# One set of quantising scales per strip, its stages divided and placed anew, and early copies moved to ScalarE, in the first layer of a two-layer kernel

## The chip, the cores and the metric

The kernel runs on one core of one Trainium2 chip. The metric is the device time of one execution in microseconds (us), the median of several runs. Five engines work side by side, each with its own queue of instructions: PE (TensorE, matmuls and transposes; its weight loads are shown apart as PEld), DVE (VectorE), ACT (ScalarE), POOL (GpSimd) and SP (SyncE, which issues transfers here).

## The reference

Two layers run one after the other on an input of 2 x 2048 tokens with 256 features. The change is in the first. It adds to the input a gated linear attention and a linear map with quantised operands, both of the normalised input; the second layer (an attention with position biases, and eight experts of which each token takes two) isn't touched. Cut to the first layer:

```python
def _gla_scan(q, k, v, g):
    def step(S, inp):
        qt, kt, vt, gt = inp
        S = jnp.exp(gt)[..., None] * S + kt[..., None] * vt[..., None, :]
        ot = jnp.einsum('bhd,bhde->bhe', qt, S)
        return (S, ot)
...
def _L0_attn_ref(x, W_in, W_out, W_g1, W_g2, ln_w):
    u = x @ W_in.T
    v, q, lg = jnp.split(u, 3, axis=-1)
    q = jax.nn.silu(q)
    f = jax.nn.sigmoid(lg)
    k = 1.0 - f
    g = jax.nn.log_sigmoid(lg)
    o = _gla_scan(tohead(q), tohead(k), tohead(v), tohead(g))
    gate = jax.nn.sigmoid(x @ W_g1.T @ W_g2.T)
    o = o * gate
    mu = jnp.mean(o, axis=-1, keepdims=True)
    var = jnp.var(o, axis=-1, keepdims=True)
    o = (o - mu) * jax.lax.rsqrt(var + LN_EPS) * ln_w
    return o @ W_out.T
...
def _mx_quantize(t, eps=1e-30):
    blocks = t.reshape(rows, K // BLOCK_SIZE, BLOCK_SIZE)
    scales = jnp.maximum(jnp.max(jnp.abs(blocks), axis=-1) / FP6_E2M3_MAX, eps)
    q = _nearest_on_grid(blocks / scales[..., None], _GRID)
    return (q, scales)
...
xn = _layernorm(x, axis=-1)
x = x + _L0_attn_ref(xn, ...) + _L0_ffn_ref(xn, ...)
```

Blocks of 32 neighbouring values share a scale: their greatest absolute value divided by 7.5. Each value divided by its scale is rounded to the nearest point of a six-bit grid and multiplied by the scale again, for the input and for the weight of the linear map.

## The kernel before

**Strips.** `layer0` (L517) works through the 4096 tokens in eight strips of 512, four to each of the two sequences. A strip's tokens lie as four tiles of 128 tokens by 256 features. An object `Strip` holds what belongs to one strip, and its methods issue the work of one step:

- `norm_x` normalises the input into `xn` (two buffers): statistics L133, L135, the power on POOL L142, the result L144; `columns_x` transposes it on PE into `xnT`.
- `values_gates` (L640) multiplies `xnT` by a joint weight, one 128x512 PSUM tile `vf_ps` for each of four token tiles. Its first half is the values, copied to `v` by ACT (L653); its second half the logits, copied to `logit` by DVE (L652). After each second tile, ACT takes Exp (L656) and Ln (L657) of two tiles together into `soft`.
- `queries_begin` and `queries_end` make the queries: `q_ps` and `c_ps` on PE, `ls` and `spans` on ACT, `arg` (L705) and `q` (L708) on DVE.
- `keys` subtracts the logits from `k_ps` (DVE, L727) and takes Exp (ACT, L730) into `kt`; `key_columns` transposes `kt` into `k_tr` on PE and copies it to `k` by DVE (L764), 128x512 for each of two heads.
- `gates` and `gates_end` make the gate (`g1T` and L748 to L750 on ACT).
- `weights` makes the products `a_ps` of keys and queries and masks them (DVE, L786).
- `chunk(n)`, n from 0 to 3, runs the recurrence over 128 tokens: `o_ds_ps` on PE, the new `state` (DVE, L844; ACT L842 where a sequence begins), `kept` (ACT, L809), the gated result `og` (DVE, L853) and its statistics.
- `norm_o`, `columns_o`, `sum_up`, `norm_2`, `columns_2` normalise and transpose the result, add both maps to the input (`y_ps` on PE, L882 on DVE) and prepare what the second layer reads: `queries_keys`, `values`, `greatest`.

**Quantising.** `mx_steps` (L163) quantises 512 values per partition, half a strip: scales on DVE (the reduction L182 to `amax`, L184 `scale`, L186 `rscale`, L188 `nscale`), then on DVE the division L190, the power of two L194 and L197, and two roundings L199 and L202, then POOL L205. This first stage ends with a `yield`. The second stage is L207 on DVE and L208 on POOL, with another `yield`; the third is L210 on DVE and L211 on POOL, which multiplies by `nscale` and leaves the result in `mx_v`. Work tiles `pw`, `r` and `nr` have one buffer each, `nscale` and `mx_v` two. `Strip.quantise` (L659) runs the two halves one after the other. Between them is no `yield`: a step that ends the first half also does the scales and the first stage of the second. So five steps do a strip. `quantised_columns` transposes the result on PE into `xdT`. The weight is quantised once, by the same stages, at the start (`quantised_weight`, L602).

**Order.** The loop at L926 writes out by hand which step follows which: strip `now` runs through its recurrence while strip `after` is prepared, `later` is normalised and `before` is handed to the second layer. `next(quantise)` marks where one step of quantising is put. PE's instructions are kept in this order (`keep_in_program_order`, named `pin`). On the other engines only pinned instructions stay in order among themselves: L207, L210 and `arg` L705 always; in `quantise(begin=pin)`, for strips 0 and 1, also the reduction L182; and for the first `norm_x` calls the first statistics. The framework's scheduler places the others by its own reckoning of when they are ready, with the source order as priority, so that DVE's rows in the trace stand among each other in another order than in the source.

**Where the steps of quantising stand.** Strip 0: the first after `keys`, the second after `key_columns`, the third after `weights`, the fourth after strip 1's `values_gates`, the fifth after `chunk(0)`. Strip 1, in the pass of strip 0: one after `quantised_columns` (before `chunk(2)`), one after `queries_end`, one after `chunk(3)`, one after `keys`, the last after `gates`. Later strips, in the pass of the strip ahead of each: after `values_gates`, after `chunk(0)`, after `chunk(1)`, after `queries_end`, after `chunk(3)`.

## Time and profile before

| | |
|---|---|
| median of 3 runs | 1642.38 us (1642.37 to 1642.56) |
| profiled execution | 1642.09 us |
| its span, first to last instruction | 1640.3 us |
| first layer, to the last `norm_ps` | some 433 us |
| busy: PE / PEld / DVE / ACT / POOL | 1583.8 / 1297.9 / 730.3 / 743.9 / 391.2 us |
| mean granted TensorE clock | 0.989 |
| the chain that ended last | PE 86%, DVE 9%, POOL 2%, ACT 1% |

The profile gives each group of instructions by source line, engine and operation, with the tile that it writes and those it reads. What the change touches, between 22 and 150 us:

| row | mean |
|---|---|
| DVE L182 `mx_amax`, 128x16 from 128x512 | 669 ns |
| DVE L190 `mx_v`, 128x512 | 686 ns |
| DVE L652 `logit`, 128x256 from PSUM | 415 ns |
| DVE L764 `k`, 128x512 from PSUM | 672 ns |
| ACT L653 `v`, 128x256 from PSUM | 370 ns |
| ACT L589 `xnT`, 128x512 from PSUM | 586 ns |
| ACT L656 `soft`, Exp, 128x512 from SBUF | 633 ns |

In rows of time, the first number is the start in us from the span's start, the second the duration. Square brackets give how long the engine was idle ahead of an instruction and what ended that wait. The chain of waits is followed back from the last instruction, at each step to what released it. A row that ends in `x8` stands for eight instructions in a row.

### The profile page before, as it was taken

The numbers are of one execution on the slowest core, as the hardware profiler recorded it, in microseconds if no ns is written. First come the engines' busy times: TensorE is split into PE (matmuls) and PEld (weight loads), VectorE is DVE, ScalarE is ACT, GpSimd is POOL, SyncE is SP. The second block draws the span as 40 slices with busy tenths as digits, with TensorE's granted clock in tenths as the row PEclk, the third lists the DMA queues.
The fourth block names the chain that finished last, engine by engine and source line by source line (L and its number), as shares of the span: only waits on it lengthen the run. The fifth ranks groups of instructions, "written<-read, shape, count | busy, mean of one in ns | idle before, by whom it ended". The sixth has DMA issues, their size and how long they took to land.

```text
span 1640.3 us, 33123 instructions
## 1 busy us (share of the span) xinstructions
PE 1583.8 (97%) x13786; PEld 1297.9 (79%) x13786; DVE 730.3 (45%) x2274; ACT 743.9 (45%) x1445; POOL 391.2 (24%) x350
## 2 busy tenths in 40 slices
PE   7789999999999999999999999999999999999996
PEld 4556676667688887888888888988898898888886
DVE  7888676664478866444353222222222222222221
ACT  4344554653688888998987211111111111111110
POOL 4333222211200003233331122222222232222221
PEclk9999999999899999999999999999999999999998
DMA  9710111313540402621126555555565565556531
GB/s 268 187 38 29 54 53 43 93 45 80 149 57 3 84 13 66 142 65 62 58 97 246 180 177 177 180 183 174 180 205 198 164 215 195 171 170 196 177 90 19
DMA packets 82511, 204.42 MB, mean 125 GB/s; under 512 B 8624, under 2 KB 64304, under 8 KB 71728
## 3 DMA queue, kind: packets, MB, share of 16 engines
q0 software_dynamic: 24944, 138.33, 26.0%
q1 hardware_dynamic: 56304, 62.71, 14.2%
q8 instruction: 110, 1.80, 0.5%
q10 hardware_dynamic: 1104, 1.18, 0.2%
q14 instruction: 49, 0.40, 0.1%
HBM read 152.26 MB, written 49.92 MB: 123 GB/s over the span
## 4 chain that ended last, share of the span: by engine, by line
PE 86%; DVE 9%; POOL 2%; ACT 1%; DMA 1%; issue 1%; POOLq 0%; SPq 0%; DVEq 0%; ACTq 0%
PE h_ps L2206 29%; PE y_ps L2222 14%; PE sc L1801 12%; PE o_ps L1823 10%; PE vf_ps L533 3%; PE y_ps L533 3%; PE f_ps L1785 2%; PE tr L583 2%; PE vg_ps L533 2%; PE qk_ps L533 1%; PE g_ps L533 1%; PE q_ps L533 1%; PE o_tr L1758 1%; PE o_ds_ps L533 1%; PE x_ps L2184 1%
## 5 line engine op out<-in xcount | busy, mean ns | idle before, releaser
L2206 PE MATMUL h_ps<-va,qk 128*128 128x256 f32 (+1 forms) x2368 | 484.5, 365 | 0.0
L2206 PEld LDWEIGHTS h_ps<-va,qk 128*128 128x128 f32 x2368 | 425.6, 190 | 53.6 <-issue 0.3
L1807 ACT ACTIVATE pt<-sc,shift 128x512 f32<-128x512 f32 (+3 forms) x687 | 403.8, 704 | 52.3 <-ACT pt L1807 27.1
L2211 ACT ACTIVATE sg<-h_ps 128x256 f32<-128x256 f32 (+1 forms) x296 | 109.2, 369 | 600.5 <-PE h_ps L2206 592.9
L2212 DVE TENSOR_TENSOR larger<-sg,h_ps 128x256 f32<-128x256 f32 (+1 forms) x296 | 119.2, 403 | 359.1 <-ACT sg L2211 359.1
L1801 PE MATMUL sc<-qk 32*128 32x128 f32 (+6 forms) x3916 | 222.5, 336 | 1.6 <-PE norm_ps L533 1.1
L1801 PEld LDWEIGHTS sc<-qk 32*128 32x128 f32 x3916 | 184.1, 186 | 35.3 <-ACT pt L1807 17.0
L1823 PE MATMUL o_ps<-pt,va 128*32 128x128 f32 (+6 forms) x3916 | 188.3, 319 | 3.4 <-DVE o_sb L114 3.4
L1823 PEld LDWEIGHTS o_ps<-pt,va 128*32 128x32 f32 x3916 | 140.6, 110 | 34.3 <-issue 9.6
L2231 POOL DMA_INDIRECT out<-va,to x69 | 109.9, 1592 | 211.0 <-DMA out<-va,to 85.4
L114 DVE TENSOR_TENSOR pt<-pt,keepmask 128x128 f32<-128x128 f32 (+3 forms) x546 | 119.7, 276 | 73.7 <-ACT pt L1807 71.8
L2222 PE MATMUL y_ps<-qk,larger 128*128 128x256 f32 x560 | 124.6, 379 | 0.1
L2227 DVE SCALAR_TENSOR_TENSOR va<-y_ps,wt,half_bias 128x256 f32<-128x256 f32 x69 | 30.4, 479 | 208.5 <-PE y_ps L2222 208.5
L2222 PE MATMUL y_ps<-larger 128*128 128x256 f32 x544 | 120.4, 379 | 0.0
L2222 PEld LDWEIGHTS y_ps<-qk,larger 128*128 128x128 f32 x560 | 104.7, 190 | 13.8 <-DVE larger L2212 0.5
L2222 PEld LDWEIGHTS y_ps<-larger 128*128 128x128 f32 x544 | 102.0, 190 | 13.1
L2116 POOL DMA_INDIRECT table<-rows,place x64 | 67.7, 1057 | 186.0 <-DMA table<-rows,place 149.4
L2146 POOL DMA_INDIRECT qk<-in_wgateup,wrow x37 | 36.7, 991 | 190.4 <-PE h_ps L2206 157.7
L533 PE MATMUL vf_ps<-qk,xnT 128*128 128x512 f32 x128 | 59.2, 617 | 0.0
L533 PEld LDWEIGHTS vf_ps<-qk,xnT 128*128 128x128 f32 x128 | 24.4, 196 | 29.6 <-issue 27.3
L114 DVE COPY o_sb<-o_ps 128x256 f32<-128x256 f32 x64 | 26.9, 422 | 42.1 <-PE o_ps L1823 41.8
L2146 POOL DMA_INDIRECT qk<-in_wdown,wrow x19 | 18.4, 968 | 110.2 <-PE y_ps L2222 83.6
(248 smaller groups left out, 1712.2 us busy)
## 6 DMA issues: line engine op xcount, KB each, us to landing
xb<-table SPq DMA_DIRECT2D x32, 265.0 KB
qk<-qk SPq DMA_DIRECT2D x32, 256.0 KB
qk<-qk SPq DMA_DIRECT2D x64, 128.0 KB
table<-spare SPq DMA_DIRECT2D x3, 2120.0 KB
va<-v SPq DMA_DIRECT2D x4, 1208.0 KB
v<-v SPq DMA_DIRECT2D x8, 574.0 KB
normed<-xn SPq DMA_DIRECT2D x8, 512.0 KB
rows<-normed POOLq DMA_DIRECT2D x16, 256.0 KB, 3.3
```

The costliest lines, as they stand in the source:

```text
L114: return lambda *a, **k: self.tc.keep_in_program_order(begin(*a, **k))
L533: tc.keep_in_program_order(nc.tensor.matmul(*args, **kwargs))
L1801: nc.tensor.matmul(scs[r][:, at : at + q1 - q0], lhsT=heads[rows, 1, kb * P : (kb + 1) * P], rhs=heads[rows, 0, qt * QT + q0 : qt * QT + q ...
L1807: nc.scalar.activation(pt[:, r, 0:width], scs[r][:, 0:width], AF.Exp, bias=shift)
L1823: nc.tensor.matmul(o_ps[r * HR : (r + 1) * HR, to + q0 : to + q1], lhsT=values[b, way][:, kb, h * VC : h * VC + HR], rhs=pt[:, r, at : at ...
L2116: self.nc.gpsimd.indirect_dma_start(out=self.c.table, in_=rows[:, n, :], in_offset=None, out_offset=bass.IndirectOffsetOnAxis(ap=to[:, 2 * ...
L2146: e.nc.gpsimd.indirect_dma_start(out=w, out_offset=None, in_=e.a[name], in_offset=bass.IndirectOffsetOnAxis(ap=e.c.wrow[:, self.b : self.b ...
L2206: nc.tensor.matmul(ps[:, j, rows], lhsT=self.wgu[:, j, c, f * P : (f + 1) * P], rhs=self.xT[:, c, rows], start=c == 0, stop=c == 1,)
L2211: nc.scalar.activation(sg, ps[:, 0, rows], AF.Silu)
L2212: nc.vector.tensor_tensor(self.hT[:, f, rows], sg, ps[:, 1, rows], ALU.mult)
L2222: nc.tensor.matmul(ps[:, c, :], lhsT=self.hT[:, fc, c * P : (c + 1) * P], rhs=self.wd[:, fc, :], start=fc == 0, stop=fc == NFC - 1,)
L2231: nc.gpsimd.indirect_dma_start(out=out, out_offset=bass.IndirectOffsetOnAxis(ap=self.to[:, c : c + 1], axis=0), in_=y[:, c, :], in_offset= ...
```

## The change

Three things change, all in the first layer.

- The scales leave `mx_steps` and become a function of their own, `mx_scales`. For a strip they are made once, for all 1024 values per partition (32 blocks), and each half takes its part. `rscale` now has two buffers. The weight's scales are made as before. What `begin` pins in `mx_steps` is now the division, and in `mx_scales` the reduction.
- `Strip.quantise` has a step of its own for the scales, and a `yield` between the halves, so that seven steps do a strip: scales, then three stages for each half. The loop's `next` calls are placed for them. Strip 0: scales and first stage after `keys`, and after `weights` both the end of the first half and the first stage of the second; the rest stands as before. Strip 1: scales after `quantised_columns`, the first half's stages after `queries_end` and after `chunk(3)` and, with the first stage of the second half, after `keys`; the last two after `gates`. Later strips: scales and first stage after `values_gates`, second stage after `chunk(0)`, third after `chunk(1)`; the second half's stages after `queries_end`, after `chunk(3)` and after `norm_o`.
- For strips 0, 1 and 2 (`early`) ACT copies the logits and the transposed keys, in place of DVE, and takes Exp of each tile straight from PSUM, four of 128x256 instead of two of 128x512.

```diff
+def mx_scales(nc, pool, src, begin=lambda ins: ins):
+    nb = src.shape[1] * E // 32
     amax = pool.tile([P, nb], F32, tag="mx_amax", name="mx_amax")
-    begin(nc.vector.tensor_reduce(amax, blocks(x), AX.X, ALU.max, apply_absolute_value=True))
+    blocks = src.rearrange("p c e -> p (c e)").rearrange("p (b k) -> p b k", k=32)
+    begin(nc.vector.tensor_reduce(amax, blocks, AX.X, ALU.max, apply_absolute_value=True))
     scale = pool.tile([P, nb], F32, tag="mx_scale", name="mx_scale")
     nc.vector.tensor_scalar(scale, amax, 1.0 / 7.5, 1e-30, ALU.mult, ALU.max)
-    rscale = pool.tile([P, nb], F32, tag="mx_rscale", name="mx_rscale")
+    rscale = pool.tile([P, nb], F32, tag="mx_rscale", name="mx_rscale", bufs=2)
     nc.vector.reciprocal(rscale, scale)
     nscale = pool.tile([P, nb], F32, tag="mx_nscale", name="mx_nscale", bufs=2)
     nc.vector.tensor_scalar(nscale, scale, -1.0, None, ALU.mult)
-    nc.vector.tensor_tensor(
+    return rscale, nscale
+
+def mx_steps(nc, pool, src, v, scales, pin=lambda ins: ins, begin=lambda ins: ins):
...
+    rscale, nscale = scales
+    begin(nc.vector.tensor_tensor(
         blocks(v), blocks(x), rscale.unsqueeze(2).to_broadcast([P, nb, 32]), ALU.mult
-    )
+    ))
...
+            self.early = s < 3
...
-                nc.vector.tensor_copy(self.logit[:, n, :], ps[:, E:])
-                nc.scalar.copy(self.v[:, n, :], ps[:, 0:E])
+                if self.early:
+                    nc.scalar.activation(self.soft[:, n, :], ps[:, E:], AF.Exp, scale=-1.0)
+                    nc.scalar.copy(self.v[:, n, :], ps[:, 0:E])
+                    nc.scalar.copy(self.logit[:, n, :], ps[:, E:])
+                else:
+                    nc.vector.tensor_copy(self.logit[:, n, :], ps[:, E:])
+                    nc.scalar.copy(self.v[:, n, :], ps[:, 0:E])
                 if n % 2:
                     part = self.soft[:, n - 1 : n + 1, :]
-                    nc.scalar.activation(part, self.logit[:, n - 1 : n + 1, :], AF.Exp, scale=-1.0)
+                    if not self.early:
+                        nc.scalar.activation(
+                            part, self.logit[:, n - 1 : n + 1, :], AF.Exp, scale=-1.0
+                        )
                     nc.scalar.activation(part, part, AF.Ln, bias=1.0)
 
-        def quantise(self, **how):
+        def quantise(self, begin=lambda ins: ins):
             self.xd = []
+            scales = mx_scales(nc, p1, self.xn, begin)
+            yield
             for i in range(2):
                 v = p1.tile([P, 2 * E], F32, tag="mx_v", name="mx_v", bufs=2)
                 self.xd.append(v.rearrange("p (c e) -> p c e", e=E))
-                for _ in mx_steps(
-                    nc, p1, self.xn[:, 2 * i : 2 * i + 2, :], v, pin, **how
-                ):
-                    yield
+                nb = 2 * E // 32
+                yield from mx_steps(
+                    nc, p1, self.xn[:, 2 * i : 2 * i + 2, :], v,
+                    [t[:, i * nb : (i + 1) * nb] for t in scales], pin, begin,
+                )
+                yield
...
-                nc.vector.tensor_copy(self.k[:, h, :], ps.rearrange("p n t -> p (n t)"))
+                copy = nc.scalar.copy if self.early else nc.vector.tensor_copy
+                copy(self.k[:, h, :], ps.rearrange("p n t -> p (n t)"))
...
     now.keys()
     next(quantise)
+    next(quantise)
     now.gates_end()
...
         now.weights()
         if not before:
             next(quantise)
+            next(quantise)
         if after:
             after.values_gates()
         if before:
             quantise = after.quantise() if after else iter(())
+            next(quantise, None)
         next(quantise, None)
         now.chunk(0)
         next(quantise, None)
         now.chunk(1)
-        if before:
-            next(quantise, None)
-        else:
-            for _ in quantise:
-                pass
+        next(quantise, None)
...
         now.norm_o()
         if before:
+            next(quantise, None)
             before.queries_keys()
         else:
             after.keys()
             next(quantise)
+            next(quantise)
             after.gates()
-            for _ in quantise:
-                pass
+        for _ in quantise:
+            pass
         now.columns_o()
```

## The prediction

> **What bounds the kernel now.** I first split the profiled execution (1642.09 us; its span is 1640.3) into the stages of the first layer. The stretches view gives, for each, PE busy, PEld, DVE, ACT, POOL (all us), then the granted clock.

> ```profile
> 21.00:54.00 33.00, 30.96 (x167) 20.83 (x166) 27.37 (x66) 20.81 (x46) 11.85 (x9) 1.00 0.97 257
> 54.00:89.00 35.00, 27.38 (x143) 21.00 (x142) 29.67 (x81) 12.77 (x25) 12.68 (x10) 0.85 0.45 122
> 89.00:147.40 58.40, 50.35 (x229) 33.88 (x229) 50.97 (x151) 24.25 (x51) 19.29 (x15) 0.94 0.11 40
> 147.40:196.40 49.00, 47.42 (x250) 33.69 (x250) 35.46 (x97) 25.94 (x54) 13.10 (x10) 1.00 0.13 45
> 294.30:342.20 47.90, 47.50 (x251) 33.77 (x252) 30.47 (x85) 26.07 (x55) 9.73 (x8) 1.00 0.23 72
> ```

> From 147 us on PE is busy 96 to 99% of each strip, and the rest of the kernel is PE too (97% of the span). Between 54 and 147 us PE idles 7.6 + 8.1 us, at a granted clock of 0.85 and 0.94, while DVE is busy 85 to 87%. So a gain can come from there almost alone. Next, the chain of waits in that stretch: it runs on DVE and POOL, and PE appears again only at 86.16.

> ```profile
> 66.09 0.61 DVE mx_r L207
> 66.77 1.38 POOL mx_r L208
> 68.17 0.69 DVE mx_nr L210
> 68.86 0.61 DVE mx_amax L182
> 69.49 0.60 DVE mx_scale L184
> 70.11 0.25 DVE mx_rscale L186
> 70.41 0.70 DVE mx_v L190
> ...
> 76.99 0.70 DVE mx_nr L210
> ...
> 79.56 1.03 POOL ln_rstdx L142
> 80.62 1.38 DVE xn L144 x4
> 82.00 0.66 DVE ln_st L133 x2
> 82.74 0.57 DVE k L764
> 83.41 0.57 DVE k L764
> ...
> 86.16 1.64 PE tr L583 x8
> ```

> Both things that the change takes off DVE, the second half's scales and the key copies, stand on this chain. Last, PE's own rows with the waits ahead of them:

> ```profile
> 47.49 0.49 PE L533 MATMUL o_ds_ps<-state,q 128*128 128x128 f32 x2 [1.25 <-ACT state L842]
> 111.33 0.49 PE L533 MATMUL o_ds_ps<-state,q 128*128 128x128 f32 x2 [3.86 <-DVE state L844]
> 167.57 0.49 PE L533 MATMUL o_ds_ps<-state,q 128*128 128x128 f32 x2 [1.28 <-DVE state L844]
> 216.63 0.49 PE L533 MATMUL o_ds_ps<-state,q 128*128 128x128 f32 x2 [1.73 <-DVE state L844]
> ```

> PE waits for the recurrence's state, and DVE is late with it because it holds stages of the quantising ahead of it.

> **A, to 54 us.** Strip 1's four logit copies (DVE, 0.42 each) no longer stand between `vf_ps` and ACT. Now ACT's last `v` copy starts at 46.28, 2.3 us after PE's last `vf_ps`, and state L842 behind it ends at 47.4. ACT's new work per `vf_ps` tile is an Exp, a `v` copy and a logit copy of 128x256 from PSUM. The nearest row, `v<-vf_ps`, is 0.37, so 3 x 0.37 + half an Ln of 0.63 = 1.43 us, under the 1.72 us in which PE makes a tile (four matmuls, 7.1 us for 16). An Exp of this shape is not in the trace: its bounds are 0.26 (spacing of the piped `v` copies) and 0.63 (the Exp of 128x512), and I take the copy's 0.37. ACT keeps pace, and PE's wait of 1.25 us goes. Against it, strip 0's two key copies (0.58 each by `xnT<-tr`, the same shape) join ACT at 34 us, where it is full from 31.2 to 36.7 with gates and `xnT`, for which PE's `vf_ps` at 37.05 waits. Cost 0 (if they fall behind `xnT`, `a_ps` then waits) to 1.16; I take 0.4. **A = -1.25 + 0.4 = -0.85**, bounds -1.3 to +1.2.

> [...] No run here shows the new Exp yet.

> **B, 54 to 89 us.** Scales: per half reduce 0.67, scale 0.17, reciprocal 0.25, negation 0.11. One set for 1024 elements instead of two: the wide reduce is not in the trace; it lies between 0.67 (free width) and 1.34 (double), I take 1.27 (+0.6), the 32-wide rest as before. So strip 1's chain loses the second set, from 68.78 to 70.40, 1.6 us, and DVE pays 0.6 earlier, near 52, where it has 0.21 us idle and is otherwise full: net -1.0. The first half's stage (L190, L194, L197, L199, L202: 2.9 us, from 53.89) moves from in front of chunk 2 to behind `queries_end`. State n=2, run at 56.15 although its `ds_ps` is done at 54.36, can go about 1.5 us earlier, and with it og. DVE's work up to L207 at 66.0 stays the same sum; the wait of 1.07 us for POOL's `rstdo` at 64.4 can now be filled by that stage. I take -0.9, so that L207 comes that much sooner; bounds -1.5 and +4.2 (all of the 2.9 and the 1.27 of POOL L205 exposed). This cost is zero only because L205, done at 58.44, waits 7.6 us for its reader now; without that cover it is the 4.2. Key copies of strip 1: 0.57 x 2 leave the chain, and ACT, idle from 69.1 to 79.5 us, takes them when `k_tr` ends at 77.5: -1.2. **B = -1.0 - 0.9 - 1.2 = -3.1**, bounds -5 and +3.

> **C, 89 to 147 us.** Here DVE is the bound, 87% busy with long waits in it (L207 takes 2.39 at 100.75 beside POOL's `acc` of 2.36; nscale 1.14 at 109.28 beside POOL L205). Off DVE go four logit copies (1.65), two key copies (1.28), a set of small scale steps (about 0.5): 3.4 us. In source the second half's stage now stands behind chunk 2 and the query tail. The unpinned rows of DVE do not follow the source (an `mx_amax` for a later strip stands at 110.34, just ahead of state at 110.94), so I grant only that state, ready from about 106, passes L202, nscale and amax (0.67 + 1.14 + 0.6 = 2.4 of the 3.86 us wait). A shorter wait also keeps PE's clock: the first 8 `qk_ps` after it take 5.29 us, the next 8 3.60; I take 0.8 of the 1.7. Of the 3.4 us I count 0.8 on top, since the last copies (139.3) are behind the transpose that PE waits for. **C = -2.4 - 0.8 - 0.8 = -4.0**, bounds -8 (all of PE's idle) and 0.

> **D, 147 to 390 us.** PE idle: 1.58, 1.72, 1.81, 0.40, 1.08 us in five strips, 6.6 in all. Each strip has DVE waiting for POOL L211 ahead of nscale (0.94 at 164.99), as its two buffers are both in use; with one nscale per strip the buffer is free long before. But L202 waits for the same POOL row through `nr`. If state passes the L202, scale and amax rows (165.07 to 166.48) the wait goes; if not, a wide amax costs 0.6 more. I take -0.8 in each of three strips: **-2.5**, bounds +3 and -5. No DMA is moved, and SP and POOL's queue get nothing new. POOL L205 may come closer to `rstdo` (172.31), 5.1 us after it is free now: covered.

> **Sum.** -0.85 - 3.1 - 4.0 - 2.5 = -10.4: 1642.1 - 10.4 = 1631.7. The median of the runs is 0.3 above the profiled execution, so 1632; for pieces that overlap (an idle gap closes once) I take 1 off the gain: **1633**.

> **Rivals.** (1) *The moves come to nothing*: DVE's order stays by readiness, only removed work counts. A -0.85, B -1.0 - 1.2, C -2 (logits and small steps), D 0: -5, **1637**. For it: the floating rows named above. Against: in strip 1 the stages are pinned. (2) *Nothing reaches PE*: what DVE saves is idle elsewhere, ACT takes 0.4; **1641.5**. Against it: key copies and scales stand on the chain itself. (3) *Slower: the late second half.* Stages stand behind `queries_end`, on DVE ahead of og's normalising. In strip 0 the uncovered 4.2 us; in each of six later strips the whole stage of 2.9 instead of the 1.7 that stands there now (L188 to L182, 164.99 to 166.48, rounded up): +1.2 x 6 = 7.2. With A and the sure gains of B (-3.0): +8.4, **1650**. It decides when the `tr` of og starts over 20 us after the last `vf_ps` of a strip; strip 1's takes 18.9 now (156.34 to 175.21). For it: og's last piece (175.53) already stands behind an L207. Against: DVE has 13 us idle in such a strip.

> **How the numbers follow.** Forecast 0.52 (its own range 1626 to 1637), rival 1 0.20, rival 2 0.08, rival 3 0.20. A measurement here can tell about 0.2%, 3.3 us, from no change; forecast and rival 1 are faster by more: 0.72; rival 2 is within: 0.08; rival 3: 0.20. The range reaches from 1625 to 1645: below it lie C and D at their bounds together, above it most of rival 3.

> **What would show it.** Strip 0: PE's `tr` of `xn2` at 86.16 comes near 82; the chain has no `k` L764 row before it. PE's 1.25 us wait for L842 is gone, and the 3.86 us one is under 2. By 147.4 some 8 us are gained; the later strips take under 49 us each. I am wrong if ACT, not PE, ends the `vf_ps` stretches, if L207 of strip 1's first half comes after 66 us, or if the time after the first layer changes its length.

## The result, and the profile after

| | before | after |
|---|---|---|
| median, same chip | 1642.55 us (1642.1 to 1646.11, 12 runs) | 1643.26 us (1639.32 to 1648.44, 12 runs) |
| profiled execution: run / span | 1642.09 / 1640.3 us | 1644.31 / 1642.5 us |

The ratio after to before is 0.9993, with a 95% interval of 0.9982 to 1.0005: no change that this kernel's measurement can tell. The forecast was 1633 us. The page of the changed kernel, its span, TensorE's work, the granted clock in 40 slices and the chain that ended last:

```profile
span 1642.5 us, 33089 instructions
...
PE 1587.1 (97%) x13786; PEld 1300.2 (79%) x13786; DVE 719.9 (44%) x2224; ACT 751.5 (46%) x1469; POOL 389.7 (24%) x350
...
PEclk9899999999899999999999999999999999999998
...
PE 89%; DVE 7%; POOL 2%; DMA 1%; issue 1%; ACT 1%; POOLq 0%; SPq 0%; DVEq 0%; ACTq 0%
```

VectorE did lose 10.4 us of work and ScalarE gained 7.6 (from 730.3 and 743.9). The end did not follow. The same stretches as in the prediction, cut at this kernel's strips (columns: length, busy us of PE, PEld, DVE, ACT, POOL, then the granted clock):

```profile
21.00:54.00 33.00, 31.97 (x181) 22.19 (x180) 24.28 (x56) 22.82 (x55) 12.57 (x9) 1.00 0.97 252
54.00:88.50 34.50, 25.21 (x125) 19.71 (x125) 27.92 (x77) 12.51 (x24) 13.13 (x10) 0.80 0.49 131
88.50:145.10 56.60, 48.73 (x230) 33.75 (x227) 46.84 (x136) 26.80 (x59) 19.81 (x15) 0.97 0.12 42
145.10:194.00 48.90, 47.98 (x251) 33.77 (x250) 34.23 (x93) 26.02 (x54) 13.04 (x10) 1.00 0.13 45
290.40:339.30 48.90, 47.98 (x249) 33.77 (x248) 30.21 (x81) 26.07 (x54) 9.59 (x8) 1.00 0.23 70
```

The first stretch is better (PE 31.97 of 33 us). In the second PE still idles 9.3 us and its clock is lower than before (0.80, it was 0.85). The third is 1.8 us shorter. The later strips are longer: 48.90 where the strip at 294 us took 47.9.

To place the difference, the table gives the start of each strip's first `a_ps` matmul, of the second layer's first `sc` matmul and of the last part's first `h_ps`, in us from the first instruction. "Later strips" is from strip 2's `a_ps` to `sc`.

| profile | strip 0 | strip 1 | strip 2 | `sc` | strip 1 takes | later strips | `sc` to `h_ps` |
|---|---|---|---|---|---|---|---|
| before | 35.16 | 87.73 | 147.32 | 434.43 | 59.59 | 287.11 | 459.08 |
| before, again (r_before) | 34.70 | 87.49 | 147.88 | 435.07 | 60.39 | 287.19 | 457.48 |
| after | 34.43 | 87.27 | 145.09 | 432.62 | 57.82 | 287.53 | 463.36 |
| after, again (r_after) | 34.29 | 87.11 | 144.92 | 432.38 | 57.81 | 287.46 | 459.27 |
| after, again (r2_after) | 33.52 | 86.34 | 144.16 | 430.69 | 57.82 | 286.53 | 457.43 |

The first layer gave 1.8 us in the pair of profiles at hand, and 1.8 to 4.4 over all pairs of these five. Part of that is the start ahead of strip 0's `a_ps`, which varies from one execution to the next: over the 17 profiles of this document it came anywhere from 33.44 to 35.24 us, and the same order of work up to there gave 33.52 us in r2_after and 35.10 in e_fill. Counted from strip 0's `a_ps` to `sc`, the change gave 1.1 us in this pair and 1.1 to 3.2 over all pairs. The second layer has the same instructions in the same order on every engine, and its length differs by 6 us between executions of one program (457.43 to 463.36). What little the first layer gave is lost in that.

### The profile page after: what moved, and what is told of

Its sections match the earlier page's. It is cut to its first block, busy times and chain, and to the rows that moved or that the text cites. A ratio compares the mean times of both kernels' runs of the same rounds, so it can differ in the third digit from the quotient of the medians.

```text
span 1642.5 us, 33089 instructions
## 1 busy us (share of the span) xinstructions
PE 1587.1 (97%) x13786; PEld 1300.2 (79%) x13786; DVE 719.9 (44%) x2224; ACT 751.5 (46%) x1469; POOL 389.7 (24%) x350
## 4 chain that ended last, share of the span: by engine, by line
PE 89%; DVE 7%; POOL 2%; DMA 1%; issue 1%; ACT 1%; POOLq 0%; SPq 0%; DVEq 0%; ACTq 0%
PE h_ps L2229 29%; PE y_ps L2245 14%; PE sc L1824 12%; PE o_ps L1846 10%; PE vf_ps L540 3%; PE y_ps L540 3%; PE f_ps L1808 2%; PE tr L590 2%; PE vg_ps L540 2%; PE g_ps L540 2%; PE qk_ps L540 1%; PE q_ps L540 1%; PE o_tr L1781 1%; PE o_ds_ps L540 1%; PE x_ps L2207 1%; PE k_ps L540 1%
## 5 line engine op out<-in xcount | busy, mean ns | idle before, releaser
L1824 PE MATMUL sc<-qk 32*128 32x128 f32 (+6 forms) x3916 | 226.0, 337 | 2.0 <-PE norm_ps L540 1.1
```

Of the source, the lines that this page charges most:

```text
L1824: nc.tensor.matmul(scs[r][:, at : at + q1 - q0], lhsT=heads[rows, 1, kb * P : (kb + 1) * P], rhs=heads[rows, 0, qt * QT + q0 : qt * QT + q ...
```

## The experiments

All times are against the kernel before on the same chip, in four comparisons, whose medians for the kernel before were 1639.1, 1638.93, 1641.14 and 1642.83 us. The ratios are those on record; the quotient of the two medians differs from them by up to 0.0013.

| kernel | median us | ratio to before, 95% | strip 1 at | strip 1 takes | later strips | `sc` |
|---|---|---|---|---|---|---|
| e_copies | 1639.87 | 1.0001 (0.9991, 1.0011) | 85.72 | 58.45 | 287.09 | 431.26 |
| e_nocopies | 1644.53 | 1.0025 (1.0013, 1.0038) | 91.50 | 59.69 | 287.54 | 438.73 |
| e_strip1 | 1636.98 | 0.9975 (0.9963, 0.9987) | 85.15 | 57.81 | 286.46 | 429.42 |
| e_later | 1635.45 | 0.997 (0.996, 0.9981) | 87.73 | 59.08 | 283.15 | 429.96 |
| e_both | 1633.68 | 0.9958 (0.9945, 0.997) | 85.23 | 57.89 | 283.01 | 426.13 |
| e_fill | 1638.1 | 0.9986 (0.9977, 0.9994) | 87.93 | 56.56 | 286.46 | 430.95 |
| r2_after | 1639.4 | 0.9991 (0.9982, 1.0001) | 86.34 | 57.82 | 286.53 | 430.69 |
| e_scales | 1639.39 | 0.9991 (0.9981, 1.0) | 87.92 | 62.06 | 283.34 | 433.32 |
| e_best | 1631.55 | 0.9939 (0.9925, 0.9953) | 85.38 | 58.00 | 281.91 | 425.29 |
| e_pin | 1627.68 | 0.9916 (0.9901, 0.9932) | 85.55 | 50.37 | 286.01 | 421.93 |
| e_after_pin | 1639.14 | 0.9981 (0.9971, 0.9991) | 86.71 | 49.98 | 294.55 | 431.24 |
| e_before_pin | 1639.46 | 0.9972 (0.996, 0.9984) | 87.35 | 51.24 | 290.55 | 429.14 |
| e_top | 1629.98 | 0.9915 (0.9898, 0.9933) | 86.61 | 50.34 | 285.49 | 422.44 |

**Both kernels once more, and the parts alone.** r_before and r_after are the two kernels unchanged, in a later comparison, one run each (1641.15 and 1640.19 us).

> The kernel before once more, for a second profile of it. First theory: the first layer repeats itself (first score matmul of the second layer at 434.4 us, within 0.5), and the second layer, the same instructions in the same order in both kernels, varies by some us from one execution to the next (1205.9 us from that matmul to the end in the first profile). Rival: the second layer is as steady as the first, and takes 1205.9 within 0.5 again.

> The changed kernel once more. First theory: first score matmul at 432.6 us within 0.5; the stretch behind it, 1209.9 us in the first profile with PE at half its clock near 848 us, may be 3 us shorter this time. Rival: the shorter first layer makes the second layer's weight gathers meet PE there, every time: 1209.9 again, within 1.

From `sc` to the end they took 1204.3 and 1206.0 us, where the first profiles had 1205.9 and 1209.9: the second layer varies by itself, and the rival of r_after falls. r_before's `sc` came 0.64 us later than in the first profile, a little more than its theory allowed.

e_copies is the kernel before with only the ScalarE copies; e_nocopies is the changed kernel without them:

```diff
-            self.early = s < 3
+            self.early = False
```

> The kernel before, with the copies of the first three strips on ScalarE alone. If the copies made the gain of the first stretch (PE's wait of 1.25 us for the first state) and of the stretch near 140 us, and the moved stages cost time, the second strip's a_ps starts at about 86.0 us (87.7 before, 87.3 with the whole change), the third's at 145 or less, and the first score matmul at 432 or less. If the scales and moves made the gain, a_ps of the second strip stays at 87.5 or later, and the score matmul at 434.

> The whole change without the copies (all copies stay on VectorE). First theory: PE's wait of 1.25 us for the first state is back, the second strip's a_ps starts at 89 us or later, the first score matmul at 435 or later, so the moved stages alone lose. Rival (scales and moves gain): score matmul at 433 or less.

Without the copies the scales and moves together cost 3.7 to 4.3 us at `sc` and 0.25% of the time. So part of the change works against the rest, and the next kernels put its placements back one by one. In the profile of e_copies `sc` comes 3.2 to 3.8 us earlier, while its ten runs show nothing. Strip 0's `a_ps` came at 33.44 us there, the earliest of all; counted from it the gain is 1.5 to 2.6 us. Its mean granted clock was 0.9893 against 0.9906 for the kernel before in the same comparison, which at about 1 us for each 0.001 (the slope below) is worth some 1.3 us. That these two are all of the difference isn't shown.

**Strip 1's first stage.** In the changed kernel's chain of waits (start, length) the moved first stage, L197 to L209, is now woven between the four `og` pieces, and the first half's `mx_r` L214 waits for GpSimd L212 right behind it:

```profile
60.45 0.60 DVE mx_v L197
...
61.21 1.21 POOL ln_rstdo L142
...
62.44 0.41 DVE og L144
62.85 0.34 DVE mx_pw L204
63.18 0.32 DVE og L144
63.51 0.60 DVE mx_r L206
64.11 0.32 DVE og L144
64.43 0.61 DVE mx_nr L209
...
65.18 1.32 POOL mx_r L212
66.50 0.02 issue
66.52 0.70 DVE mx_r L214
```

e_strip1 puts that stage back ahead of chunk 2:

```diff
             next(quantise)
+            next(quantise)
         now.chunk(2)
...
         next(quantise, None)
+        if not before:
+            next(quantise)
         now.norm_o()
...
             after.keys()
             next(quantise)
-            next(quantise)
             after.gates()
```

> The changed kernel with strip 1's first quantising stage back ahead of strip 0's third chunk, the second behind the queries, the third and the second half's first behind the fourth chunk; scales, copies and the later strips as changed. Theory (the moved first stage is what lost the strip 0 stretch: strip 1's L214 of the first half began at 66.52 us in the changed kernel's trace, where the prediction wanted 62): that L214 begins near 64, TensorE's idle ahead of the transposes of the quantised columns (2.35 us at 78.46) falls to about 1, strip 1's first a_ps matmul moves from 87.27 to about 85.5 us and the second layer's first sc from 432.6 to about 430.9. Rival (the wide amax and ScalarE's copies lost it): a_ps stays at 87.3 within 0.4 and the time is that of the changed kernel.

Rows of time of e_strip1, in the same place (in brackets, idle time ahead and what ended it):

```profile
63.32 1.03 PE L590 MATMUL tr<-ident,og 128*128 128x128 f32 x3 [2.98 <-DVE og L144]
...
64.33 0.68 DVE L214 SCALAR_TENSOR_TENSOR mx_r<-mx_r,mx_pw 128x512 f32<-128x512 f32 x1
64.93 0.41 DVE L144 TENSOR_SCALAR og<-og,ln_mvo,ln_rstdo 128x256 f32<-128x256 f32 x1
65.10 1.37 POOL L215 TENSOR_TENSOR mx_r<-mx_r,mx_pw 128x512 f32<-128x512 f32 x1 [2.37 <-DVE mx_r L214]
```

L214 starts 2.2 us earlier, because L212 ran at 55.51, long before it is read. PE's wait for `og` falls from 4.55 to 2.98 us, its wait for the quantised columns from 2.4 to 0.2, and strip 1 starts at 85.15, as the theory said. The rival falls. (The 62 us in that text stands nowhere in the prediction; its terms, 66.01 - 0.85 + 0.6 - 0.9, put this row near 65.)

**The later strips.** In strip 5 of the changed kernel, the second half's first pass stands ahead of the norm, so GpSimd's queue holds L215 when `ln_veo` is ready:

```profile
313.85 0.68 DVE L214 SCALAR_TENSOR_TENSOR mx_r<-mx_r,mx_pw 128x512 f32<-128x512 f32 x1
...
314.52 0.16 DVE L140 TENSOR_SCALAR ln_veo<-ln_mvo 128x4 f32<-128x4 f32 x1
314.61 1.28 POOL L215 TENSOR_TENSOR mx_r<-mx_r,mx_pw 128x512 f32<-128x512 f32 x1 [4.49 <-DVE arg L727]
315.83 1.03 POOL L142 TENSOR_TENSOR ln_rstdo<-ln_veo,expo 128x4 f32<-128x4 f32 x1
316.90 0.74 DVE L144 TENSOR_SCALAR og<-og,ln_mvo,ln_rstdo 128x256 f32<-128x256 f32 x2 [2.21 <-POOL ln_rstdo L142]
```

e_later gives the strips from 2 on their places of before:

```diff
         now.chunk(1)
         next(quantise, None)
+        if before:
+            next(quantise, None)
...
         if before:
-            next(quantise, None)
             before.queries_keys()
```

> The changed kernel with the stages of the strips from 2 on placed as in the kernel before (first two passes after chunk 1, the second half's first pass after the queries, its second after chunk 3); strip 1, scales and copies as changed. Theory (in each later strip GpSimd's L215 of the second half stands ahead of the norm's ln_rstdo and holds og's transposes): strips 4 and 5 take 48.6 and 49.3 us or less from a_ps to a_ps again by losing about 1.0 us each, the waits of TensorE for og fall from 0.59 to 0.41 or less, and the first sc comes at about 430.5 us instead of 432.6. Rival (the strips after 2 are bound by TensorE's own work): every strip within 0.3 us of the changed kernel's 48.90, 47.11, 49.31, 48.90, 48.89.

The same place in e_later:

```profile
313.51 1.02 POOL L142 TENSOR_TENSOR ln_rstdo<-ln_veo,expo 128x4 f32<-128x4 f32 x1 [3.96 <-DVE ln_veo L140]
314.57 1.06 DVE L144 TENSOR_SCALAR og<-og,ln_mvo,ln_rstdo 128x256 f32<-128x256 f32 x3 [1.00 <-POOL ln_rstdo L142]
...
316.90 1.37 POOL L215 TENSOR_TENSOR mx_r<-mx_r,mx_pw 128x512 f32<-128x512 f32 x1 [2.37 <-DVE mx_r L214]
317.20 0.76 PE L590 MATMUL tr<-ident,og 128*128 128x128 f32 x5 [0.41 <-DVE og L144]
```

`ln_rstdo` goes first again and VectorE waits 1.00 us for it, not 2.21. Strips 2, 4, 5 and 6 take 47.75, 48.17, 47.74 and 47.75 us, each 1.14 to 1.16 less than after: 4.6 us together, while strip 1 takes 1.3 more. The theory holds.

**Both undone.**

> Both placements as before, so that only the scales made at once and the ScalarE copies are left of the change. Theory: the two gains add, the first sc at about 429 us, and the whole at the same granted clock about 3.5 us (0.2%) under the changed kernel. Rival one: the time of the changed kernel within 0.1%, because what the first layer gives is lost again to the clock. Rival two: the first sc at 432 or later.

At `sc` it is 6.5 us under the changed kernel, 3 us more than the theory wanted, and 8.3 to 8.9 under the kernel before. e_scales is e_both with `self.early = False`:

> Only the scales made at once, with every stage where the kernel before has it and no copies on ScalarE (of the parts: e_both without the copies). Theory: the scales are worth 5.1 us by e_copies and e_both (first sc 431.26 and 426.13) and without the copies about the same: first sc at 429 to 431 us, the time about 0.9975 of the kernel before. Rival (they pay only once VectorE is rid of its copies): first sc at 433 or later, the time within 0.1% of before.

Here the rival held: the scales alone give 1.1 to 1.8 us at `sc`, the copies alone 3.2 to 3.8, both 8.3 to 8.9. Counted from strip 0's `a_ps` (35.06, 33.44 and 34.35 us) it is 1.0 to 2.1, 1.5 to 2.6 and 7.5 to 8.6, and in the time 0.9991, 1.0001 and 0.9958. In e_scales strip 1 takes 62.06 us against 57.89 with the copies: a wide set of scales pays there only once VectorE is rid of its copies.

**The rows that float.** In strip 1 of the changed kernel VectorE does a later strip's `xn`, reduction and scale between chunk 0 and state:

```profile
95.71 1.38 DVE L144 TENSOR_SCALAR xn<-acc,ln_mvx,ln_rstdx 128x256 f32<-128x256 f32 x4 [1.70 <-POOL ln_rstdx L142]
...
97.34 1.20 DVE L168 TENSOR_REDUCE mx_amax<-xn 128x32 f32<-128x1024 f32 x1
...
98.79 0.77 DVE L170 TENSOR_SCALAR mx_scale<-mx_amax 128x32 f32<-128x32 f32 x1
...
100.47 0.61 DVE L866 SCALAR_TENSOR_TENSOR state<-o_ds_ps,to_next,kept 128x128 f32<-128x128 f32 x2
100.88 0.49 PE L540 MATMUL o_ds_ps<-state,q 128*128 128x128 f32 x2 [2.58 <-DVE state L866]
```

e_pin is e_both with strip 3's statistics pinned:

```diff
-            later.norm_x(**({} if before else {"begin": pin}))
+            later.norm_x(**({} if s > 1 else {"begin": pin}))
```

> e_both with strip 3's norm statistics pinned behind strip 1's normed columns, so that its rows can't float ahead of the state passes. Theory (floated rows hold the state passes in strip 1, TensorE idles 2.57 and 2.19 us for state at 96 and 107 us): the state waits of strip 1 fall by 2 us or more together and strip 2's a_ps comes 2 us earlier, at about 141. Rival (the rows only move to a place where they hold og or the norm instead): strip 2's a_ps at 143 or later, because the 4 xn rows and the statistics are then late for strip 3's columns.

In e_pin state runs at once, VectorE having stood idle ahead of it, and PE goes on to `q_ps` with no wait:

```profile
95.95 0.61 DVE L866 SCALAR_TENSOR_TENSOR state<-o_ds_ps,to_next,kept 128x128 f32<-128x128 f32 x2 [5.43 <-PE o_ds_ps L540]
...
97.13 3.17 PE L540 MATMUL q_ps<-xnT,qk 128*128 128x512 f32 x7
```

Strip 1 takes 50.37 us instead of 57.89, far more than the theory's 2 (PE's idle time there falls from 8.04 to 2.44 us, and its clock goes from 0.97 to 1.00); strip 2 gives 2.6 back (50.36 for 47.75). At 0.9916 (0.9901, 0.9932) this is 0.4% faster than e_both and, by medians, 13.5 us under the kernel before. Two kernels more make the same edit in the changed kernel and in the kernel before:

> The changed kernel with strip 3's norm statistics pinned behind strip 1's normed columns, nothing else. Theory (in strip 1 the floated rows of later strips, not the change's own stages, took the expected gain of the state passes): strip 1, a_ps to a_ps, falls from 57.8 us by 5 to 8, strip 2 loses up to 3 of it, the first sc comes at 427 to 429 us and the time is 0.995 to 0.997 of the kernel before. Rival (the pinning pays only with the stages put back): first sc at 431 or later and the time within 0.1% of the changed kernel's.

> The kernel before with the same pinning alone. Theory (the floated rows held strip 1 in the kernel before as well, where TensorE waited 3.86 us for state at 107 us): strip 1 falls from 59.6 us by 4 or more and the first sc comes at 431 or earlier. Rival (before the change those rows stood in time nobody needed): strip 1 within 1.5 us of 59.6, the time within 0.1% of before; then the loss in strip 1 of the changed kernel is one that the change made.

So the floated rows held strip 1 in the kernel before too: there it falls from 59.6 to 51.2 us, though strip 2 then takes 52.64. In the changed kernel it falls as much (57.82 to 49.98), but strip 2 rises from 48.90 to 55.64, with a wait for state of 3.80 us at 147.7, and `sc` comes at 431.24, not at 427 to 429. The edit pays in full only with the stages put back.

```profile
76.22:79.63 3.41, 0.88 (x6) 0.64 (x6) 3.08 (x13) 0.98 (x3) 1.85 (x3) 1.00 0.00 0
79.63:86.46 6.83, 5.75 (x18) 4.55 (x19) 5.59 (x18) 2.93 (x6) 3.86 (x3) 0.50 0.00 0
120.59:124.00 3.41, 1.86 (x10) 1.37 (x11) 3.02 (x9) 0.96 (x3) 0.62 (x2) 1.00 0.21 77
124.00:127.41 3.41, 3.41 (x10) 2.71 (x9) 2.97 (x7) 1.29 (x3) 1.79 (x2) 0.50 0.02 5
```

PE idles 2.53 and 1.55 us in one step, and the next, in the first case the next two, run at 0.50. e_fill adds TensorE work that no result needs into such waits:

```diff
+    def fill(out, count):
+        for _ in range(count):
+            tc.keep_in_program_order(nc.tensor.transpose(out, ident, ident))
...
             for n in range(4):
+                fill(ps[:, n, :], fills.get((e, n), 0))
                 tc.keep_in_program_order(
```

> The changed kernel with extra TensorE work that no result needs, put where TensorE waits in its trace: 7 transposes of the identity inside the quantised columns of strip 1 (idle 2.35 us there), 4 ahead of strip 2's columns (1.37), 8 ahead of strip 1's normed columns (2.50), and strip 6's norm rows made 5 and 4 times (1.39 and 0.86); nothing else changes its order on any engine. In the six traces at hand the granted clock halves for steps of 3.41 us, and every step of that grid in which TensorE idled over 1.86 us was followed by a halved one, none under 1.3 us that began at full clock. Theory (these idle times, not the work, cost the clock): the halved stretches at 79.6 to 86.5, 124.0 and 417.6 us are gone, the mean granted clock rises by about 0.004 and the time falls by 3 to 5 us, although TensorE does about 7 us more work. Rival (the clock is lost for another reason, such as the power of the work): the same stretches stay, or others take their place, and the time is that of the changed kernel or up to 4 us more.

Its stretches near 120 us:

```profile
118.79:122.21 3.42, 2.20 (x12) 1.20 (x10) 1.75 (x10) 3.17 (x6) 2.25 (x2) 1.00 0.41 154
122.21:125.62 3.41, 2.48 (x13) 1.83 (x14) 3.41 (x9) 1.15 (x2) 0.80 (x1) 1.00 0.23 81
```

Between 29 us and the end of the work six steps are halved, against 9, 8 and 6 in the three profiles of the changed kernel; the one at 124 and the one at 417 are gone (but one of the three profiles of the changed kernel, r2_after, has none at 417 either), the one near 80 is one step long instead of two, and one at 101.7 came new. Over the runs the mean clock rose from 0.9895 (both sets of the changed kernel) to 0.9918 (the kernel before beside e_fill: 0.9904; beside r2_after: 0.9898), and the ratio to the kernel before went from 0.9991 and 0.9993 to 0.9986, whose interval overlaps theirs: the mean clock rose with the idle time filled, but a gain in time isn't shown here. The same on e_both and on e_pin:

> e_both with extra TensorE work that no result needs where TensorE waits in its trace: 9 transposes of the identity ahead of strip 0's normed columns (idle 2.98 us there), 4 ahead of strip 2's columns (1.37), 4 ahead of strip 1's normed columns (1.15), strip 6's norm rows made 5 and 4 times (1.39 and 0.86). Order on every engine else as in e_both. Theory (idle steps of 3.41 us halve the next): the halved stretches that began at 62.98, 80.05, 121.0 and 411.1 in e_both's trace are gone or shorter, the mean granted clock rises by 0.003 or more and the time falls by 2 to 4 us below e_both's, to 0.993 to 0.995 of the kernel before. Rival (the clock goes by another cause): the time of e_both or more, and as many halved stretches.

> e_pin with extra TensorE work that no result needs where it waits: 9 transposes of the identity ahead of strip 0's normed columns, 4 ahead of strip 2's columns, strip 6's norm rows made 5 and 4 times. Theory (idle steps halve the next): the halved stretches at 63.2 and 407.9 us are gone, the mean granted clock is 0.994 or more and the time 1 to 3 us under e_pin's. Rival: e_pin's time or more.

e_best: three halved steps instead of seven, mean clock 0.9936 for 0.9898, ratio 0.9939 for 0.9958, 0.2%, with intervals that overlap a little. e_top: three instead of five (the two near 64 us, at which the nine transposes were aimed, stay), 0.9945 for 0.9920, and no gain (0.9915 for 0.9916). Whether the added work takes back what the clock gives there isn't shown; each has four runs.

> The changed kernel as it is, beside the others on one chip. Theory (the milestones belong to the program, the rest is the clock): a_ps of strip 1 at 87.1 to 87.9 us, the first sc within 2 us of 432.5, and the run times spread over 5 us or more along the granted clock, about 0.9 us for each 0.001 of it. Rival (the first layer itself differs by several us from one execution to the next): the first sc is over 2 us away from 432.5.

The first layer kept within 2 us of the other profiles of the changed kernel, strips 0 and 1 within 0.02 us in length; strip 1's `a_ps`, at 86.34, missed the theory's 87.1 because strip 0 started early (33.52 us). Over its 11 runs the time spread by 5.6 us, about 1.3 us for each 0.001 of mean clock; over the runs of the kernel before in the four comparisons the slope was 0.97 to 1.08.

## Why the prediction was wrong, point by point

**What bounds it** was right in part. The experiments on the order gained by taking VectorE or GpSimd rows from ahead of a PE wait, and the largest single piece, the 7.5 us of e_pin, lies in strip 1. But "a gain can come from there almost alone" was too narrow: of the 8.3 us by which e_both is ahead at `sc`, 4.1 come from strip 2 on, where PE was called busy 96 to 99%.

**A (-0.85) was right.** PE's wait of 1.25 us for state is 0.24, and the gain stood at 1.7 us by 47 us. Of that 0.73 stood at strip 0's `a_ps` already, which is within the spread of the start; 0.96 came behind it. The row with the wait, and ScalarE's new rows between 22 and 150 us (mean ns behind the busy time):

```profile
45.25 0.49 PE L540 MATMUL o_ds_ps<-state,q 128*128 128x128 f32 x2 [0.24 <-ACT state L864]
...
L786 ACT COPY k<-k_tr 128x512 f32<-128x512 f32 x6 | 3.3, 588 | 8.1 <-PE k_tr L783 8.0
L674 ACT ACTIVATE soft<-soft 128x512 f32<-128x512 f32 x5 | 3.3, 653 | 0.0
L664 ACT COPY logit<-vf_ps 128x256 f32<-128x256 f32 x8 | 3.1, 390 | 0.0
L662 ACT ACTIVATE soft<-vf_ps 128x256 f32<-128x256 f32 x8 | 3.1, 384 | 7.0 <-PE vf_ps L540 7.0
L663 ACT COPY v<-vf_ps 128x256 f32<-128x256 f32 x8 | 2.9, 367 | 0.0
```

0.384 + 0.367 + 0.390 + half of 0.653 is 1.47 us a tile, under PE's 1.72; the forecast was 1.43. The Exp took 0.384 us, where the prediction took 0.37 from the `v` copy's row.

**B (-3.1) failed, at the moved first stage.** The lead of 1.7 us at 47 us was 0.46 at strip 1's `a_ps`. The step "I take -0.9, so that L207 comes that much sooner" is the one that failed: that row (L214 after) came at 66.52 instead of 66.01, so with the lead the move cost 2.2 us, and e_strip1 got 2.1 back. The prediction had said that the cost is zero only while GpSimd's pass waits 7.6 us for its reader, and then took the stage behind the queries without counting that this uses the cover up: L212 ran at 65.18 with VectorE waiting for it. Scales and key copies should have given 2.2 more; from that row to `a_ps` 0.97 came (21.72 to 20.75 us). The scales' rows freed 1.6 us, of which L201 took back 0.7: beside GpSimd's L218 it lasted 1.16 us, where L194 had 0.43.

```profile
69.92 1.16 DVE L201 TENSOR_SCALAR mx_pw<-mx_v 128x512 int32<-128x512 int32 x1
...
81.61 2.36 POOL L641 TENSOR_TENSOR acc<-acc,qk 128x1024 f32<-128x1024 f32 x1 [1.50 <-DVE xn L144]
...
84.08 1.02 POOL L142 TENSOR_TENSOR ln_rstd<-ln_ve,expo 128x4 f32<-128x4 f32 x1
85.13 1.38 DVE L144 TENSOR_SCALAR xn<-acc,ln_mv,ln_rstd 128x256 f32<-128x256 f32 x4 [0.72 <-POOL ln_rstd L142]
```

The key copies (-1.2) gave nothing. Both before (80.62 to 85.60) and after (80.15 to 85.13) it takes 4.98 us from the first normalising `xn` to the second, because `ln_rstd` stands on GpSimd 0.11 us behind its `acc` pass of 2.36 us, whether VectorE copies the keys meanwhile or not. From that second `xn` to `a_ps` it is 2.13 and 2.14 us. So the chain of waits that the prediction read named the copies, but they only filled the time of that pass. This is read from the two traces; no run moves the `acc` pass.

**C (-4.0) gave 1.8, and not by its main term.** "I grant only that state passes L202, nscale and amax" failed: the rows freed were taken by others that float, as the rows at 95.71 show. In strip 1 PE had waited 0.54 and 3.86 us for state; now it waited 2.58 us at 100.88 and 2.19 here:

```profile
111.23 0.49 PE L540 MATMUL o_ds_ps<-state,q 128*128 128x128 f32 x2 [2.19 <-DVE state L866]
```

In sum that is 4.8 us for 4.4, and PE's idle time in the stretch stayed what it was (8.05 us of 58.40 before, 7.87 of 56.60 after; 7.67 and 7.86 over strip 1 in r_before and r_after). The 1.8 us are its clock: the same work took PE 48.73 us for 50.35, at 0.97 for 0.94, with one halved step (at 124.0 us) for two (at 112.3 and 139.6). Of C's terms only the 0.8 for the clock came, doubled, and not by the shorter wait it was to follow from: that part is luck. The prediction had seen one such row at 110.34 and didn't ask what holding them back was worth: 7.5 to 8.4 us of strip 1, with 2.6 to 6.7 paid back in strip 2.

**D (-2.5) had the wrong sign** (+0.4), though its own step held: from strip 2 on PE's waits for state fell from 4.3 us to 0.3. But its waits for `og` rose from 1.4 to 3.7 us (1.6 in e_later). The nscale wait moved to `nr` L209, and "GpSimd's L205 may come closer to `rstdo`: covered" was the wrong row: L208 (L215 after) came ahead of `rstdo`. That is rival 3, in GpSimd's queue rather than VectorE's, at 1.15 us in each of four strips where 1.2 in each of six was priced. The term itself was there: with the stages as before, the wide scales make the later strips 283.0 to 283.3 us long (e_both, e_later, e_scales), some 4 us under the kernel before, more than the 2.5 forecast. So no single rival happened: A as forecast, with nearly half of C's amount (by the clock), is set against rival 3's price in strip 0 (2.2 of 4.2) and later.

**The sum.** Of the 10.4 us forecast 1.8 came in this pair of profiles: 0.7 ahead of strip 0's `a_ps`, -0.3 in strip 0, 1.8 in strip 1 (1.6 of it by the clock) and -0.4 from strip 2 on. By its number rival 2 (1641.5, chance 0.08) came nearest, but not for its reason: the first layer did get shorter, and the spread of the second hid it. e_both, which keeps the scales and copies but not the placements, is 8.3 us shorter at `sc` than the profile before, and 0.9958 in time, near the forecast's 0.9943. Of the marks, the `tr` of `xn2` came at 86.13 us, not near 82; both waits for state in strip 1 were over 2 us; 2.2 us were gained by strip 2's `a_ps`, not 8; and L207 of strip 1's first half came after 66 us, one of the signs of being wrong. The last mark also struck: the second layer changed its length, but the repeats show that it does so without the change.

## What to carry to other kernels

Before a stage is moved, follow its first row to the engine that reads it: here a GpSimd pass that had ended 7.6 us ahead of its reader cost 2.2 us once its writer was moved next to that reader, and another one held up the small row behind it in GpSimd's queue for 1.15 us. A row on the chain of waits is worth its time only if nothing else ends the same wait just behind it (the key copies left it, and the stretch from `xn` to `xn` kept its 4.98 us); look for the second one. Time freed on VectorE, whose order is by readiness, went to whatever floats (holding that back made strip 1 7.5 us shorter in e_pin), so hold those rows back before or together with the saving, and look at the strip that receives them. Where the single parts are measured, measure them together too: 3.5 and 1.4 us at `sc` made 8.6 here, or 2.0 and 1.6 made 8.0 counted from strip 0's `a_ps` (means over the two profiles before).

## What the runs showed of the hardware

**How much idle time halves the clock.** In all 17 profiles, from 25 us to the end of PE's work, every 3.41 us step that began at full clock is put by the time that PE idled in it, in sum: of 44 steps with 2.0 us or more, all 44 were followed by a halved one; from 1.7 to 2.0 us, 15 of 27; from 1.3 to 1.7, 20 of 50; from 1.0 to 1.3, 3 of 42; from 0.5 to 1.0, none of 146. So the bound of 1.86 us that I wrote ahead of e_fill doesn't hold as a sharp one, and its "none under 1.3 us" overlooked the step at 844.20 us shown below. The idle time was not always one wait: in 15 of the 44 steps no single wait was over 1.73 us. A halved step with over 0.5 us of idle was followed by another one each time (23 of 23), one with less in 11 of 95 cases.

**A halved step with PE nearly busy.** Below 0.5 us of idle two of some 7500 steps were followed by a halved one, both at the same place of the second layer, here in the changed kernel:

```profile
844.20:847.62 3.42, 3.13 (x39) 1.87 (x29) 1.29 (x8) 2.42 (x4) 1.95 (x2) 1.00 0.56 155
847.62:851.03 3.41, 3.41 (x47) 2.87 (x47) 2.19 (x11) 2.42 (x4) 0.00 (x0) 0.50 1.01 428
```

There 39 matmuls stand where the step before had 84, while the weight loads of the matmuls wait up to 0.45 us with no releaser in the trace, just as the first weight gathers of the last part begin. The second layer took 463.36 and 463.46 us in these two executions and 457.4 to 460.2 in the other fifteen. That the gathers cause it was not tried; they don't do it alone, for in r_after the first ones were issued at the same time (844.26 us, here 844.29) and 82 matmuls stand in the same 3.4 us. The cause stays open.
